# Adapter gating in a cross-attention and feed-forward kernel: once for both batches, with A through DRAM and the sums written from GpSimd's queue

## The chip, the core and the metric

The kernel runs on one core of a Trainium2 chip. The metric is the device time of one execution in microseconds (us), median of several. The engines are TensorE (PE, with its weight loads PEld), VectorE (DVE), ScalarE (ACT), GpSimd (POOL) and SyncE (SP). Each works through its own list of instructions in order, and they wait for each other by semaphores. SP, ACT and POOL can also issue DMAs; 16 DMA engines carry them all.

## What is computed

For two batches of 1024 tokens by 2048 features, all float32:

```python
x = x + fake_quant(layernorm(x)) @ fake_quant(ctx)              # ctx: 2048 x 2048 per batch
z = layernorm(x)                                                # viewed as 8 groups of 256 tokens
A_eff = einsum('bn,nri->bri', gate, lora_A)                     # gate 8 x 16, lora_A 16 x 32 x 2048
B_eff = einsum('bn,nor->bor', gate, lora_B)                     # lora_B 16 x 2048 x 32
x = x + z @ kernel + bias + (z @ A_eff.T) @ B_eff.T + (z @ A_sh.T) @ B_sh.T
```

There are eight groups of tokens (`GB` = 8), four to a batch (`GPB` = 4), and each has its own gate. So each has its own sums over the 16 adapters, `A_eff` and `B_eff` (32 x 2048). The change concerns how these sums are formed and moved.

## The kernel before

The kernel does one batch (`for b in range(B)`) after the other. A batch has two halves.

**Attention half.** The tokens of a group, two tiles of 128, are `y[g]`. `prep_x` (L277) normalises and quantises a tile and transposes it into `c1T[g]`. The context is worked in four blocks `n` of 512 columns. SP loads it in pieces of 512 KB into the small buffers `lit` (ten of 512 KB). `quantise` (L310) turns a piece into bf16 in `c2[n]`: ACT writes an int16 buffer `q2b` (three of them, L314), DVE clips it into a big buffer (L317), and the `lit` buffer goes back. `column_term` (L327) forms a correction for the block (`pcp` and `pc` on PE). `xattn_pair(b, n, g)` (L350) is a pair of tiles against a block: ACT starts the two halves of a PSUM tile `pa` with the column term (L359), PE adds 2 x 16 matmuls (L361), and DVE adds the result to `y` (L370) and takes its statistics (L372). Three such PSUM tiles go round.

**Adapters.** The adapters lie with 16 adapters x 8 ranks on 128 rows, so that `gmat`, 128 rows by (group, rank), sums over the adapters in one matmul. `gated` (L376) does this for one batch and one block of 512 columns: two loaded buffers of two pieces each, four matmuls with 32 columns of weights (4 groups x 8 ranks) into four row ranges of one PSUM tile `pg` (L383), and a copy into a `q2b` buffer by DVE (L395). Then `lora_a_step` (L398) transposes the sums on PE (`pga`, four transposes, L403), and DVE copies them into `acat` (L406), the weights of the later product `px`. `lora_b_step` (L411) writes the sums to DRAM, `bd[b]`, by eight DMAs of 32 KB on SP's queue (L416). Both are done for each batch, A for block 0 to 3 and then B for block 0 to 3. The A steps stand between the quantises of block 2 and the pairs of block 2. B step 0 stands ahead of the pairs of block 3 and the others between them. The PSUM pool `ps_m` has two buffers; `pg`, `pga`, `pcp`, `pc`, `ptz`, `pt` and `px` take turns in it.

The pieces of context and adapters come in one list, `todo`, in the order of use. Each time a buffer of `lit` is given back, `load_next` issues the next ones of the list on SP, up to nine ahead, and not those of batch 1 before batch 0's last stage.

**Feed-forward half.** When the pairs of block 3 are through, `prep_z` (L422) normalises `y` into z (DVE, L428), transposes it (PE, `ptz`, L432; ACT copies, L433) and stores it to DRAM. `lora_ax` (L442) multiplies z with `acat` (PE, `px`, L448, two tiles of 64 columns; ACT copies it to `axT`, L456). Then z times `kernel` runs as a fast matrix product: seven outer products of sums of blocks, each of seven inner ones (L611, the matmuls `fu`, `fv`, `fw`). The sums of weights are DVE's (L551, L560), those of z POOL's. Between them `Delta.step` (L466) adds the adapters' second product: ACT loads `bp` from `bd` (L473) and a row of `bias` into the one buffer `bias_b` (L476), starts a PSUM tile `pl` from it (L478), PE adds `axT` times `bp` (L483) and DVE adds that to `y` (L493).

In the last outer product of batch 0 the first stages of batch 1 are put between the inner products (`meanwhile`, L803).

A scheduler orders each engine's instructions from the dependencies and its own costs; only the DVE instructions that pass through `line` (L499) are held in the written order.

Of the kernel before, what the change touches and what calls it, by code (L numbers as in the profile page):

```python
# [10 lines left out]
F32 = mybir.dt.float32  # L11
# [55 lines left out]
def tile_quant_xattn_then_lora_ffn(  # L67
# [30 lines left out]
    H = D // 2  # L98
    KH = KT // 2
    KQ = KT // 4  # L100
    GP = GPB * RC

    const = ctx.enter_context(tc.tile_pool(name="const", bufs=1))
    small = ctx.enter_context(tc.tile_pool(name="small", bufs=4))
# [15 lines left out]
    bp = Bufs([const.tile([P, NB], F32, tag=f"bp{i}", name=f"bp{i}") for i in range(2)])  # L120
    bias_b = Bufs([const.tile([P, NB], F32, tag=f"bias{i}", name=f"bias{i}") for i in range(1)])
    axT = const.tile([P, GPB // 2, GT], F32, tag="axT", name="axT")
    gmat = const.tile([P, 2, GPB // 2, RC], F32, tag="gmat", name="gmat")
    st1 = const.tile([P, MT, NN, 6], F32, tag="st1", name="st1")
    st2 = const.tile([P, MT, NN, 6], F32, tag="st2", name="st2")
    r_s = const.tile([P, MT], F32, tag="r_s", name="r_s")
# [4 lines left out]
    ]  # L131


    bd = [dram.tile([GPB, 2, R, D], F32, tag=f"bd{b}", name=f"bd{b}") for b in range(B)]

    def bf(t, n):

# [2 lines left out]
    def flat(t):  # L140
        return t.rearrange("p k n -> p (k n)")
# [14 lines left out]
    for b in range(B):  # L156
        for n in range(2):
            todo.extend((b, raw_src(b, n, r)) for r in range(KT // 2))
        for n in range(2, 4):
            for r in range(KT // 2):  # L160
                todo.append((b, raw_src(b, n, r)))
                if r in ((3, 7) if n == 2 else (5, 7)):
                    todo.extend((b, ad_src(la, 2 * (n - 2) + r // 6 if n == 3 else r // 4, h)) for h in range(2))
        for n in range(NN):
            todo.extend((b, ad_src(lb, n, h)) for h in range(2))
    loaded = deque()
    ahead = [2]
# [14 lines left out]
    def next_loaded():  # L182
        return loaded.popleft()
# [59 lines left out]
    )  # L243
    gval = const.tile([P, GB], F32, tag="gval", name="gval")
    nc.vector.tensor_tensor(gate_b, gate_b, m_ad.unsqueeze(1).to_broadcast([P, GB, NL]), ALU.mult)
    for b in range(B):
        for i in range(2):
            nc.vector.tensor_reduce(
                gval[:, ds(b * GPB + i * 2, 2)], gate_b[:, b * GPB + i : (b + 1) * GPB : 2, :], AX.X, ALU.add
            )  # L250

    def norm_stats(stats, name):
# [68 lines left out]

    colt = {}
    pairs = []

    def column_term(b, n, c2):  # L327

# [21 lines left out]
    def xattn_pair(b, n, g, c1T, c2):  # L350

        cols = ds(n * NB, NB)
        pairs.append((b, n, g))
        pa = ps_acc.tile([P, MG, NB], F32, tag=("acc0", "acc1", "delta")[len(pairs) % 3], name=f"pa_{b}_{n}_{g}")
        for j in range(MG):

            m = g * MG + j
            with tc.high_priority():
                nc.scalar.activation(pa[:, j, :], colt[n], AF.Identity, bias=r_s[:, m : m + 1])  # L359
            for k in range(KT):  # L360
                nc.tensor.matmul(  # L361
                    pa[:, j, :],
                    c1T[g][:, k, ds(j * P, P)],
                    c2[k // 8][:, k % 8, :],
                    start=False,
                    stop=(k == KT - 1),
                    skip_group_check=True,
                )
        yp = y[g][:, :, cols]
        summed = nc.vector.scalar_tensor_tensor(yp, pa, s12, yp, ALU.mult, ALU.add)  # L370
        for j in range(MG):
            nc.vector.bn_stats(st2[:, g * MG + j, n, :], y[g][:, j, cols])  # L372
        return summed


    def gated(nm):  # L376

        ps = ps_m.tile([P, NB], F32, tag="pm", name=f"pg_{nm}")
        for h in range(2):
            buf, t = next_loaded()  # L380
            for c in range(2):
                row = (2 * h + c) * GP
                nc.tensor.matmul(  # L383
                    ps[row : row + GP, :],
                    gmat.rearrange("p i a r -> p (i a r)"),
                    t[:, c, :],
                    start=True,
                    stop=True,
                    skip_group_check=True,
                )  # L390
            lit.give(buf)
            load_next()
        st = q2b.take()
        sf = st.rearrange("p k n -> p (k n)").bitcast(F32)
        nc.vector.tensor_copy(sf, ps)  # L395
        return st, sf

    def lora_a_step(b, n):  # L398

        st, sf = gated(f"a{b}_{n}")  # L400
        pt = ps_m.tile([P, KQ, P], F32, tag="pm", name=f"pga_{b}_{n}")
        for k in range(KQ):
            nc.tensor.transpose(pt[:, k, :], sf[:, ds(k * P, P)], ident)  # L403
        q2b.give(st)
        for g in range(GPB):
            nc.vector.tensor_copy(  # L406
                acat[:, ds(n * KQ, KQ), own_col[g], :].rearrange("p k (c r) -> p k c r", c=NC),
                pt.rearrange("p k (c i a r) -> p i a k c r", c=NC, i=2, r=RC)[:, g % 2, g // 2],
            )

    def lora_b_step(b, n):  # L411

        st, sf = gated(f"b{b}_{n}")
        for c in range(NC):
            for i in range(2):
                nc.sync.dma_start(  # L416
                    out=bd[b][i::2, i, ds(c * RC, RC), ds(n * NB, NB)],
                    in_=sf[ds(c * GP + i * (GP // 2), GP // 2), :],
                )
        q2b.give(st)  # L420

    def prep_z(b, m, zq, wk):  # L422

# [34 lines left out]
    class Delta:  # L458
# [7 lines left out]
        def step(self):  # L466
            if not self.units:
                return
            pr, n, j = self.units.popleft()
            cols = ds(n * NB, NB)  # L470
            if j == 0:
                self.bp, self.bb = bp.take(), bias_b.take()
                nc.scalar.dma_start(  # L473
                    out=self.bp, in_=bd[self.b][ds(2 * pr, 2), :, :, cols].rearrange("g s r n -> (g s r) n")
                )
                nc.scalar.dma_start(out=self.bb, in_=bias[cols].partition_broadcast(P))  # L476
            pl = ps_acc.tile([P, 2, NB], F32, tag="delta", name=f"pl_{self.b}_{n}_{pr}_{j}")
            nc.scalar.copy(pl, self.bb.unsqueeze(1).to_broadcast([P, 2, NB]))  # L478

            for h in range(2):  # L480
                for i in range(2):
                    rows = slice(i * 2 * R, (i + 1) * 2 * R)
                    nc.tensor.matmul(  # L483
                        pl[:, i, ds(h * (NB // 2), NB // 2)],
                        axT[rows, pr, ds(j * P, P)],
                        self.bp[rows, ds(h * (NB // 2), NB // 2)],
                        start=False,
                        stop=True,
                        skip_group_check=True,
                    )  # L490
            for i in range(2):
                yb = y[2 * pr + i][:, j, cols]
                line(nc.vector.tensor_add(yb, pl[:, i, :], yb))  # L493
            if j == MG - 1:
                bp.give(self.bp)
                bias_b.give(self.bb)
# [194 lines left out]
            big.give(t)  # L691

    for b in range(B):
        nc.vector.tensor_tensor(
            gmat.rearrange("p i a r -> p (i a) r"),
            m_rk.unsqueeze(1).to_broadcast([P, GPB, RC]),
            gval[:, ds(b * GPB, GPB)].unsqueeze(2).to_broadcast([P, GPB, RC]),
            ALU.mult,
        )
        if b == 0:  # L700
            open_c2(0)
            prep_x(0, 0, c1T, wk)
# [21 lines left out]
        for g in range(2, GPB):  # L724
            for m in range(g * MG, (g + 1) * MG):
                with tc.issue_after(opened.ins):
                    prep_x(b, m, c1T, wk)
            for n in range(2):
                xattn_pair(b, n, g, c1T, c2[n])
                if g + 1 == GPB:  # L730
                    close_c2(n)
                    open_c2(n + 2)
                    bp.give(colt.pop(n))
                    if n == 0:
                        for r in range(NR):
                            quantise(c2[2], r)
                            if r % 4 == 3:
                                lora_a_step(b, r // 4)
                        column_term(b, 2, c2[2])
        if b == 0:  # L740
            for pr in range(GPB // 2):
                nc.sync.dma_start(out=acat[:, :, 3 * pr + 1, :], in_=a_sh)
            for bb in range(B):
                for g in range(GPB):
                    nc.sync.dma_start(out=bd[bb][g, 1 - g % 2], in_=b_sh)
        for g in range(GPB):
            xattn_pair(b, 2, g, c1T, c2[2])
            for r in {0: range(3), 1: range(3, 6), 2: range(6, 8), 3: ()}[g]:
                quantise(c2[3], r)
            if 1 <= g <= 2:  # L750
                lora_a_step(b, g + 1)
            if g == 2:
                column_term(b, 3, c2[3])
        lora_b_step(b, 0)
        close_c2(2)
        bp.give(colt.pop(2))
        first = Operands(b, 0)
# [2 lines left out]
        for g in range(GPB):  # L760
# [7 lines left out]
                first.comb("t1", "b12", "b11", ALU.subtract)  # L768
            elif g == 2:
                first.load("b22")  # L770
            if g < 3:
                lora_b_step(b, g + 1)
            if g > 0:
                zqs[g - 1] = [lit.take() for _ in range(4)]
                group_z(b, g - 1, wk, zqs[g - 1])
# [134 lines left out]
```

## Time and profile before

| | us |
|---|---|
| median of three runs (1127.28 to 1128.93) | 1128.51 |
| the profiled execution | 1128.61 |
| its span, first to last instruction | 1126.8 |
| PE busy in the span | 1072.4 |
| DVE busy | 741.5 |
| POOL busy | 266.6 |
| ACT busy | 261.1 |

The granted TensorE clock was 0.999 over the span. The profile is of one execution; a time in it is counted from the span's start. Batch 0's attention half lies at about 0 to 210 us, its adapter steps at 104 to 191; batch 1's from about 590, its adapter steps at 644 to 729. A row of the groups by line gives line, engine, operation, output<-input, size and count, then busy time and mean duration of one, then the idle time before them and what ended it. A row of a timeline begins with start and length. One float32 matmul leaves two records. The chain of waits is followed back from the last instruction to what released each step.

### The profile page before, as it was taken

The page shows a single profiled execution, that of the slowest core. Times are in us where ns is not written, and L with a number is a line of the kernel's source. Part 1 is how long each engine was busy: PE and PEld are TensorE (multiplying, and loading weights), DVE is VectorE, ACT ScalarE, POOL GpSimd, SP SyncE. Part 2 cuts the span into 40 slices and gives each one's busy share as a digit, 9 for nine tenths or more (in the row PEclk, how much of TensorE's full clock was granted, in tenths as well). Part 3 has the DMA queues.
Part 4 walks back from the last instruction along what each step waited for, and adds up shares of the span by engine and source line. Part 5 has one row for each costly group of instructions (what it writes and reads, how often), then busy time and mean ns, then how long its engine had stood idle before and what let it go on. Part 6 is the DMA issues. An engine that isn't in the chain of part 4 may idle for free.

```text
span 1126.8 us, 10619 instructions
## 1 busy us (share of the span) xinstructions
PE 1072.4 (95%) x3926; PEld 489.3 (43%) x3926; DVE 741.5 (66%) x969; ACT 261.1 (23%) x342; POOL 266.6 (24%) x106
## 2 busy tenths in 40 slices
PE   1689899999999999999999999999999999999998
PEld 0244334554444444444444433455444444444443
DVE  4685547576696768568777654766668586865861
ACT  5875513320001010001375761232000000000000
POOL 0000000234253422525000000022535343243600
PEclk9999999999999999999999999999999999999999
DMA  8991935885789757489857094588668875749611
GB/s 307 391 244 35 282 124 217 298 322 205 246 285 377 266 181 264 141 301 355 285 184 228 1 277 154 182 301 314 244 215 293 295 255 181 256 145 322 213 38 56
DMA packets 120772, 261.35 MB, mean 232 GB/s; under 512 B 11920, under 2 KB 16144, under 8 KB 119568
## 3 DMA queue, kind: packets, MB, share of 16 engines
q1 hardware_dynamic: 99264, 218.65, 56.6%
q10 hardware_dynamic: 21456, 42.02, 10.5%
q8 instruction: 31, 0.51, 0.2%
q14 instruction: 21, 0.17, 0.0%
HBM read 224.99 MB, written 37.75 MB: 233 GB/s over the span
## 4 chain that ended last, share of the span: by engine, by line
PE 80%; DMA 7%; DVE 6%; ACT 4%; issue 1%; SPq 1%; ACTq 0%; DVEq 0%
PE fu L611 33%; PE fv L611 17%; PE pa L361 13%; PE fw L611 9%; DMA lit<-in_ctx_dram 4%; PE pl L483 3%; PE ptz L432 2%; DVE big L560 1%; PE pg_a L383 1%; DVE st L283 1%; PE pg_b L383 1%; ACT big L298 1%; ACT big L295 1%; DMA bd<-q2b 1%; DMA big<-in_w_dram 1%
## 5 line engine op out<-in xcount | busy, mean ns | idle before, releaser
L611 PE MATMUL fu<-big,lit 128*128 128x512 f32 x896 | 396.3, 594 | 2.4 <-DVE y L629 2.4
L560 POOL TENSOR_TENSOR lit<-lit,lit 128x1024 f32<-128x1024 f32 x56 | 165.2, 2957 | 539.4 <-PE pa L361 209.1
L611 PEld LDWEIGHTS fu<-big,lit 128*128 128x128 f32 x896 | 167.8, 190 | 208.2 <-issue 206.7
L361 PE MATMUL pa<-big,big 128*128 128x512 bf16 x1024 | 238.0, 382 | 11.9 <-ACT pa L359 10.6
L611 PE MATMUL fv<-big,lit 128*128 128x512 f32 x448 | 198.1, 594 | 0.0
L551 POOL TENSOR_TENSOR lit<-lit,lit 128x1024 f32<-128x1024 f32 x40 | 100.9, 2524 | 283.4 <-DMA lit<-zs 255.5
L560 DVE TENSOR_TENSOR big<-big,big 128x2048 f32<-128x2048 f32 x56 | 159.4, 2850 | 5.9 <-PE ptz L432 5.3
L361 PEld LDWEIGHTS <-big 128*128 128x128 bf16 x1024 | 97.0, 98 | 146.5 <-issue 44.3
L629 DVE TENSOR_TENSOR y<-y,fu 128x1024 f32<-128x1024 f32 (+1 forms) x98 | 113.7, 1194 | 67.2 <-PE fu L611 66.8
L611 PEld LDWEIGHTS fv<-big,lit 128*128 128x128 f32 x448 | 84.3, 190 | 105.0 <-issue 105.0
L629 DVE TENSOR_TENSOR y<-y,fv 128x1024 f32<-128x1024 f32 x48 | 56.8, 1218 | 91.1 <-PE fv L611 91.1
L478 ACT COPY pl<-bias 128x1024 f32<-128x1024 f32 x32 | 32.6, 1017 | 344.9 <-DVE y L493 327.1
L314 ACT ACTIVATE q2b<-lit,sc,inv 128x1024 int16<-128x1024 f32 x64 | 76.6, 1230 | 146.4 <-DMA lit<-in_ctx_dram 124.7
L551 DVE TENSOR_TENSOR big<-big,big 128x2048 f32<-128x2048 f32 x40 | 101.7, 2544 | 13.2 <-DMA big<-in_w_dram 13.2
L611 PE MATMUL fw<-big,lit 128*128 128x512 f32 x224 | 100.6, 596 | 0.1
L370 DVE SCALAR_TENSOR_TENSOR y<-pa,k_s,y 128x1024 f32<-128x1024 f32 x32 | 41.0, 1282 | 69.7 <-PE pa L361 69.7
L359 ACT ACTIVATE pa<-bp,r_s 128x512 f32<-128x512 f32 x64 | 42.8, 684 | 105.6 <-PE pa L361 60.5
L629 DVE TENSOR_TENSOR y<-y,fw 128x1024 f32<-128x1024 f32 x24 | 28.4, 1217 | 52.5 <-PE fw L611 52.5
L611 PEld LDWEIGHTS fw<-big,lit 128*128 128x128 f32 x224 | 41.3, 190 | 48.7 <-issue 48.2
L303 PE MATMUL pt<-ident_h,big 128*128 128x128 bf16 x256 | 20.3, 231 | 29.6 <-ACT big L298 29.4
L283 DVE BATCH_NORM_STATS2 st<-y 128x6 f32<-128x512 f32 x64 | 42.1, 680 | 2.9 <-DMA y<-in_x_dram 2.9
L317 DVE TENSOR_SCALAR big<-q2b 128x1024 bf16<-128x1024 int16 x64 | 27.6, 440 | 23.7 <-ACT q2b L314 20.5
(79 smaller groups left out, 609.9 us busy)
## 6 DMA issues: line engine op xcount, KB each, us to landing
big<-in_w_dram SPq DMA_DIRECT2D x96, 1024.0 KB
lit<-zs SPq DMA_DIRECT2D x88, 512.0 KB
lit<-in_ctx_dram SPq DMA_DIRECT2D x64, 512.0 KB
out_dram<-y ACTq DMA_DIRECT2D x30, 512.0 KB
zs<-lit ACTq DMA_DIRECT2D x24, 512.0 KB
y<-in_x_dram SPq DMA_DIRECT2D x8, 1024.0 KB
lit<-in_lora_a_dram SPq DMA_DIRECT2D x32, 256.0 KB
lit<-in_lora_bt_dram SPq DMA_DIRECT2D x32, 256.0 KB
```

The source lines that it names most:

```text
L283: nc.vector.bn_stats(st1[:, m, n, :], ym[:, ds(n * NB, NB)])
L314: nc.scalar.activation(qi, t, AF.Relu, bias=z2, scale=inv2)
L317: nc.vector.tensor_scalar(c2[r // 4][:, ds(2 * (r % 4), 2), :], qi, QMAX, CENTRE, ALU.min, ALU.subtract)
L359: nc.scalar.activation(pa[:, j, :], colt[n], AF.Identity, bias=r_s[:, m : m + 1])
L361: nc.tensor.matmul(pa[:, j, :], c1T[g][:, k, ds(j * P, P)], c2[k // 8][:, k % 8, :], start=False, stop=(k == KT - 1), skip_group_check=True,)
L370: summed = nc.vector.scalar_tensor_tensor(yp, pa, s12, yp, ALU.mult, ALU.add)
L478: nc.scalar.copy(pl, self.bb.unsqueeze(1).to_broadcast([P, 2, NB]))
L483: nc.tensor.matmul(pl[:, i, ds(h * (NB // 2), NB // 2)], axT[rows, pr, ds(j * P, P)], self.bp[rows, ds(h * (NB // 2), NB // 2)], start=Fal ...
L551: line(eng.tensor_tensor(got[0], got[0], got[1], ALU.add if terms[1][2] > 0 else ALU.subtract))
L560: line(eng.tensor_tensor(out_t, at[p], at[q], op))
L611: nc.tensor.matmul(ps[:, m, :], at[:, k, ds(m * P, P)], bt[:, k, :], start=(opens and k == 0), stop=(ends and k == KQ - 1), skip_group_che ...
L629: line(nc.vector.tensor_tensor(yp, yp, chains[chain][:, js, :], ALU.add if sign > 0 else ALU.subtract))
```

## The change

- `gmat` holds the gates of all eight groups (`GP` is now 8 x 8 = 64) and is formed once, ahead of the loop over batches.
- `gated` works on half a block column, one loaded buffer: two matmuls with 64 columns of weights into the two halves of a PSUM tile (L388), one copy by DVE (L399), four DMAs of 64 KB on POOL's queue (L402).
- The copy goes no longer to a `q2b` buffer, but to one of two buffers of their own, `stage`: `bias_b`'s one buffer and `axT`, whose own work begins later.
- Both A and B are gated in batch 0 alone, for both batches. The second batch's adapter loads leave `todo`.
- The sums of A go to a DRAM tensor `ad`. In each batch, ACT's queue loads them back (`load_at`, two loads of 512 KB, L422) into a `lit` buffer, and `lora_at_step` transposes them on PE (16 transposes a batch, as before) and copies them into `acat` (L437, 8 copies a batch where there were 16 of half the size). The transposes are held behind the last matmul of the latest pair.
- `bd` is one tensor for both batches. It takes the same bytes in 32 DMAs instead of 64.

```diff
...
     KQ = KT // 4
-    GP = GPB * RC
+    GP = GB * RC
...
     axT = const.tile([P, GPB // 2, GT], F32, tag="axT", name="axT")
-    gmat = const.tile([P, 2, GPB // 2, RC], F32, tag="gmat", name="gmat")
+
+    stage = Bufs([bias_b.spare[0], axT.rearrange("p g t -> p (g t)")])
+    gmat = const.tile([P, 2, GB // 2, RC], F32, tag="gmat", name="gmat")
...
-    bd = [dram.tile([GPB, 2, R, D], F32, tag=f"bd{b}", name=f"bd{b}") for b in range(B)]
+    ad = dram.tile([2, GB // 2, R, D], F32, tag="ad", name="ad")
+    bd = dram.tile([GB, 2, R, D], F32, tag="bd", name="bd")
...
                 todo.append((b, raw_src(b, n, r)))
-                if r in ((3, 7) if n == 2 else (5, 7)):
+                if b == 0 and r in ((3, 7) if n == 2 else (5, 7)):
                     todo.extend((b, ad_src(la, 2 * (n - 2) + r // 6 if n == 3 else r // 4, h)) for h in range(2))
-        for n in range(NN):
+        for n in range(NN if b == 0 else 0):
...
     nc.vector.tensor_tensor(gate_b, gate_b, m_ad.unsqueeze(1).to_broadcast([P, GB, NL]), ALU.mult)
-    for b in range(B):
-        for i in range(2):
-            nc.vector.tensor_reduce(
-                gval[:, ds(b * GPB + i * 2, 2)], gate_b[:, b * GPB + i : (b + 1) * GPB : 2, :], AX.X, ALU.add
-            )
-
+    for i in range(2):
+        nc.vector.tensor_reduce(gval[:, ds(i * GB // 2, GB // 2)], gate_b[:, i::2, :], AX.X, ALU.add)
+    nc.vector.tensor_tensor(
+        gmat.rearrange("p i a r -> p (i a) r"),
+        m_rk.unsqueeze(1).to_broadcast([P, GB, RC]),
+        gval.unsqueeze(2).to_broadcast([P, GB, RC]),
+        ALU.mult,
+    )
...
     pairs = []
+    last_mm = []
...
             for k in range(KT):
-                nc.tensor.matmul(
+                mm = nc.tensor.matmul(
...
                 )
+        last_mm.append(mm)
...
-    def gated(nm):
+    def gated(nm, n, h, dst):
         ps = ps_m.tile([P, NB], F32, tag="pm", name=f"pg_{nm}")
-        for h in range(2):
-            buf, t = next_loaded()
-            for c in range(2):
-                row = (2 * h + c) * GP
-                nc.tensor.matmul(
-                    ps[row : row + GP, :],
-                    gmat.rearrange("p i a r -> p (i a r)"),
-                    t[:, c, :],
-                    start=True,
-                    stop=True,
-                    skip_group_check=True,
-                )
-            lit.give(buf)
-            load_next()
-        st = q2b.take()
-        sf = st.rearrange("p k n -> p (k n)").bitcast(F32)
+        buf, t = next_loaded()
+        for c in range(2):
+            nc.tensor.matmul(
+                ps[c * GP : (c + 1) * GP, :],
+                gmat.rearrange("p i a r -> p (i a r)"),
+                t[:, c, :],
+                start=True,
+                stop=True,
+                skip_group_check=True,
+            )
+        lit.give(buf)
+        load_next()
+        sf = stage.take()
         nc.vector.tensor_copy(sf, ps)
-        return st, sf
-
-    def lora_a_step(b, n):
-
-        st, sf = gated(f"a{b}_{n}")
-        pt = ps_m.tile([P, KQ, P], F32, tag="pm", name=f"pga_{b}_{n}")
-        for k in range(KQ):
-            nc.tensor.transpose(pt[:, k, :], sf[:, ds(k * P, P)], ident)
-        q2b.give(st)
-        for g in range(GPB):
-            nc.vector.tensor_copy(
-                acat[:, ds(n * KQ, KQ), own_col[g], :].rearrange("p k (c r) -> p k c r", c=NC),
-                pt.rearrange("p k (c i a r) -> p i a k c r", c=NC, i=2, r=RC)[:, g % 2, g // 2],
-            )
-
-    def lora_b_step(b, n):
-
-        st, sf = gated(f"b{b}_{n}")
-        for c in range(NC):
+        for c in range(2):
             for i in range(2):
-                nc.sync.dma_start(
-                    out=bd[b][i::2, i, ds(c * RC, RC), ds(n * NB, NB)],
+                nc.gpsimd.dma_start(
+                    out=dst[i][:, ds((2 * h + c) * RC, RC), ds(n * NB, NB)],
...
                 )
-        q2b.give(st)
+        stage.give(sf)
+
+    def lora_a_step(n):
+
+        for h in range(2):
+            gated(f"a_{n}_{h}", n, h, ad)
+
+    def lora_b_step(n):
+
+        own = [bd[i::2, i] for i in range(2)]
+        for h in range(2):
+            gated(f"b_{n}_{h}", n, h, own)
+
+    def load_at(b, n2):
+
+        buf = lit.take()
+        nc.scalar.dma_start(
+            out=flat(buf),
+            in_=ad[:, ds(b * GPB // 2, GPB // 2), :, ds(2 * n2 * NB, 2 * NB)].rearrange("i a r n -> i (a r) n"),
+        )
+        return buf
+
+    def lora_at_step(b, n2, buf, behind):
+
+        t = flat(buf)
+        for n in range(2):
+            pt = ps_m.tile([P, KQ, P], F32, tag="pm", name=f"pga_{b}_{n2}_{n}")
+            with tc.issue_after(behind):
+                for k in range(KQ):
+                    nc.tensor.transpose(pt[:, k, :], t[:, ds((n * KQ + k) * P, P)], ident)
+            for pr in range(GPB // 2):
+                nc.vector.tensor_copy(
+                    acat[:, ds((2 * n2 + n) * KQ, KQ), 3 * pr : 3 * pr + 3 : 2, :],
+                    pt.rearrange("p k (i a r) -> p a k i r", i=2, r=R)[:, pr],
+                )
+        lit.give(buf)
...
                 nc.scalar.dma_start(
-                    out=self.bp, in_=bd[self.b][ds(2 * pr, 2), :, :, cols].rearrange("g s r n -> (g s r) n")
+                    out=self.bp, in_=bd[ds(self.b * GPB + 2 * pr, 2), :, :, cols].rearrange("g s r n -> (g s r) n")
...
     for b in range(B):
-        nc.vector.tensor_tensor(
-            gmat.rearrange("p i a r -> p (i a) r"),
-            m_rk.unsqueeze(1).to_broadcast([P, GPB, RC]),
-            gval[:, ds(b * GPB, GPB)].unsqueeze(2).to_broadcast([P, GPB, RC]),
-            ALU.mult,
-        )
...
                             quantise(c2[2], r)
-                            if r % 4 == 3:
-                                lora_a_step(b, r // 4)
+                            if b == 0 and r % 4 == 3:
+                                lora_a_step(r // 4)
...
                 nc.sync.dma_start(out=acat[:, :, 3 * pr + 1, :], in_=a_sh)
-            for bb in range(B):
-                for g in range(GPB):
-                    nc.sync.dma_start(out=bd[bb][g, 1 - g % 2], in_=b_sh)
+            for g in range(GB):
+                nc.sync.dma_start(out=bd[g, 1 - g % 2], in_=b_sh)
...
                 quantise(c2[3], r)
-            if 1 <= g <= 2:
-                lora_a_step(b, g + 1)
+            if b == 0 and 1 <= g <= 2:
+                lora_a_step(g + 1)
+            if g == 2:
+                at0 = load_at(b, 0)
...
                 column_term(b, 3, c2[3])
-        lora_b_step(b, 0)
+        lora_at_step(b, 0, at0, last_mm[-1].ins)
+        if b == 0:
+            lora_b_step(0)
...
                 first.load("b22")
-            if g < 3:
-                lora_b_step(b, g + 1)
+            if g == 0:
+                at1 = load_at(b, 1)
+            if g == 1:
+                lora_at_step(b, 1, at1, last_mm[-1].ins)
+            if b == 0 and g < 3:
+                lora_b_step(g + 1)
...
```

Line numbers of the instructions that the change adds (L388, L399, L402, L422, L437) are those of the changed kernel; all others are of the kernel before.

## The prediction

> **What bounds the kernel now.** I read the page's first two parts, then TensorE's (PE's) timeline around the adapter steps, then busy time by stage, the chain of waits and SyncE's (SP's) timeline.
>
> From the page:
>
> ```profile
> PE 1072.4 (95%) x3926; PEld 489.3 (43%) x3926; DVE 741.5 (66%) x969; ACT 261.1 (23%) x342; POOL 266.6 (24%) x106
> ...
> L383 PE MATMUL pg_a<-lit,gmat 128*32 128x512 f32 x64 | 14.8, 605 | 0.0
> L383 PE MATMUL pg_b<-lit,gmat 128*32 128x512 f32 x64 | 14.8, 605 | 0.0
> ```
>
> PE is 95% busy; no other engine passes 66%. So PE time taken off comes off the end, unless the next matmul then waits. (The L383 rows are from the groups by line. They overlap, so their 14.8 us are not PE's time; starts are.)
>
> PE's timeline, batch 1's first two A steps, then B step 3:
>
> ```profile
> 644.07 1.04 PE L383 MATMUL pg_a<-lit,gmat 128*32 128x512 f32 x2
> 645.04 3.63 PE L361 MATMUL pa<-big,big 128*128 128x512 bf16 x16
> 648.60 1.06 PE L383 MATMUL pg_a<-lit,gmat 128*32 128x512 f32 x6
> 649.59 2.33 PE L361 MATMUL pa<-big,big 128*128 128x512 bf16 x10
> ...
> 652.29 1.06 PE L383 MATMUL pg_a<-lit,gmat 128*32 128x512 f32 x8
> 653.29 1.47 PE L361 MATMUL pa<-big,big 128*128 128x512 bf16 x6
> ...
> 728.31 1.07 PE L383 MATMUL pg_b<-lit,gmat 128*32 128x512 f32 x8
> ```
>
> An f32 matmul leaves two records. One alone (x2) holds PE 645.04-644.07 = 0.97 us, three (x6) 0.99, four (x8) 1.00: 32-column tiles run beside each other, so the price is per group, about **0.98 us**. Each batch has 14 groups (A 7, B 7): 13.7 us.
>
> Busy time by stage (columns: stage, length, PE, PEld, DVE, ACT, POOL busy, granted clock, DMA share, GB/s):
>
> ```profile
> 116.00:134.00 18.00, 15.84 (x84) 6.91 (x83) 9.48 (x19) 11.59 (x13) 0.00 (x0) 1.00 1.06 282
> 134.00:155.00 21.00, 21.00 (x108) 8.10 (x106) 9.71 (x19) 1.81 (x3) 0.00 (x0) 1.00 0.55 149
> 155.00:179.00 24.00, 24.00 (x107) 8.29 (x105) 13.00 (x25) 4.91 (x9) 0.00 (x0) 1.00 0.52 192
> 656.00:672.00 16.00, 15.91 (x85) 6.81 (x83) 9.63 (x19) 11.56 (x13) 0.00 (x0) 1.00 1.06 286
> 693.00:717.00 24.00, 24.00 (x107) 8.44 (x106) 13.07 (x25) 4.91 (x9) 0.00 (x0) 1.00 0.54 193
> ```
>
> From 134 us and in all of batch 1 PE is full. Only at 116-134 are the DMA engines full (1.06) and PE waits: 2.16 us at 128.83, for ACT's second start of pa, which stands behind a quantise that waits for ctx. DVE is at 46 to 54% in these stages. POOL has nothing until about 200 us.
>
> **Batch 1, removed.** Its 32 gated matmuls, 8 copies (L395, 0.68 us) and 32 bd writes go: **-13.7 us** of PE. Its 8.4 MB of adapter loads go too; they only shared full DMA engines where PE did not wait (656-672). The 16 transposes of A stay (0.53 us a group of four, before and after). What is late next, from the built order of the changed kernel:
> - pcp of block 2 now stands right behind pa of pair (0,3), cut in 10+2+2+2 between pa. Such cuts of two cost 0.33 us at 595.31 (0.98 uncut at 656.28): +0.8, and +0.3 for block 3 (10+6). The quantises of 646-653 (ACT 1.16 apiece) and the statistics between them make PE wait some 1.2 us where 0.78 are idle now: +0.4.
> - PE's 1.09 us at 750.72 waits for axT, which ACT copies only after bp's load, which waits for the bd writes. No writes, no wait: -1.1. Cutting one pl in four: +0.3.
>
> Batch 1: -13.7+0.8+0.3+0.4-1.1+0.3 = **-13.0 us** (ends -11 and -14).
>
> **Batch 0, added.** (a) Two 64-column tiles replace four 32-column ones. That they run side by side, px shows (64 columns, two at a time):
>
> ```profile
> 232.64 0.43 PE L448 MATMUL px<-lit,acat 128*64 128x256 f32 x1
> 232.65 0.43 PE L448 MATMUL px<-big,acat 128*64 128x256 f32 x1
> ```
>
> The built order gives 11 slots for A (a pair, or a lone half) and 8 for B; consecutive pairs cost 0.87 each, the others 0.98: 10.6+7.5 = 18.1 us, against 13.7: +4.4, shared out below. The number of PSUM copies does not change (16 in all, now all here): +5.4 us of DVE, in its gaps of about 4 us ahead of y at L370.
>
> (b) The sums are written from POOL: 64 DMAs of 64 KB, four behind each copy, and a buffer's next copy (DVE, in order) waits until its four have landed. Behind that copy stand y's sums, quantises and z's halves on DVE, and with them PE's PSUM buffers. No row shows a DMA issued by POOL. Nearest rows, SP's own writes of these sums and two landings in the chain of waits:
>
> ```profile
> L416 SPq DMA_DIRECT2D bd<-q2b x64: 567/567/814, 161.9 to 743.7; - x64
> ```
>
> ```profile
> 724.27 2.64 DMA zs<-lit
> 727.54 6.01 DMA bd<-q2b
> ```
>
> Issue d: ends 0.35 (ACT's bp<-bd, 346 ns) and 3.9 us (SP's two acat<-in_a_sh in 7.85); the nearest row is 0.567 for 16 rows of 2 KB, and 32 rows are written now. I take 1.0, towards its double. Landing L: 2.6 to 6.0; I take 3.5.
> - A, blocks 0 and 1 (104-134). The third copy waits for the first's four: 110.9+4x1.0+3.5 = 118.4 instead of 113; pcp waits 2 us. But ACT's second start of pa now stands behind both late ctx quantises: 129.36+1.24+0.69 = 131.3 instead of 128.83, which covers that wait and the three slots added there. So +2.5, and 0.4 for two pa less done ahead: **+2.9**. Ends 0 and +6.5: 1.05 MB of sums at 282 GB/s are 3.7 us more on full DMA engines.
> - A, blocks 2 and 3: 4.8 us of slots for 3.9: **+0.9**. The load of A on ACT's queue waits for the last A write; PE has 15.6 us of work until it needs the starts behind it: nothing, unless 8d+L passes 15.
> - B (155-194): slots **+0.6**. 32 DMAs x 1.0 = 32 us fit into 39, but steps come in pairs: the last copy needs the DMAs of the pair before, 8d+L = 11.5 us after their copy, when PE has some 10 us of work between; the bias load on ACT then waits for 4d+L. Together **+3** (ends 0 at d = 0.57 and L = 2.6, +9 at 1.13 and 6.0).
> - SP's 32 bd writes no longer stand ahead of w's loads (SP, 192.52 for 13.51 us), nor ahead of axT (PE's 1.22 us at 212.47): **-0.4**, since POOL's may be as late.
>
> Batch 0: 2.9+0.9+0.6+3-0.4 = **+7.0 us** (ends +1 and +15).
>
> **Sum.** -13.0+7.0 = -6.0. The profiled execution took 1128.61 us, 1.81 around its span of 1126.8, and is 0.1 above the median of the three (1128.51): **1122.5 us**.
>
> **A rule that speaks against it.** The quantise L317 takes 440 ns for 1024 elements, z's L428 0.72 to 0.81 us; about 0.5 us of every 4 on DVE is of this kind here. The Trainium skill, "SBUF — State Buffer", on the "DVE blocks DMA" trap, says that a DMA issued from GpSimd has its descriptors written by GpSimd's cores, which DVE locks out during its two-port modes; its example goes from about 620 to 3100 ns. By that example for every DMA, an estimate, B alone would take 32x3.1 = 99 us, and the kernel would be some 60 us slower. The page "DMA: Bandwidth & Descriptors", section "Anatomy of one DMA — SWDGE (gpsimd) path", fits 2.0 us plus bytes/436e3, so 2.15 us for 64 KB: by it as L the sum would be about 2 us lower. No row here shows either.
>
> **Rivals.**
> - *All waits hidden* (24%). DVE's gaps and POOL's idle queue speak for it, the pairs against. B's 3 us vanish and axT's 1.2 go: 2.9+0.9+0.6-1.2 = +3.2, so -9.8: **1118.8**.
> - *Given back in batch 0* (13%): L = 6.0, as the bd row has it, with full engines: A 5.5+0.9, B 7.5 with its slots, no relief: -13+13.9: **1129.5**.
> - *POOL's queue is the bound: slower* (10%). 32 DMAs must pass in B's 39 us, so it decides from d = 1.22, and eats the gain from about 1.4. At three of SP's issues, 1.7 us: 32x1.7-39 = 15.4, on top of A's 3.8 and B's slots 0.6: -13+4.4+15.4: **1135.4**. For it: software's price is unseen; against: nothing else runs on POOL, and SP's 0.567.
> - *Halves run one after the other* (3%): 32x0.87 = 27.8 instead of 18.1: -6+9.7: **1132.3**. px speaks against it. That batch 1 keeps gated matmuls is excluded: its built order has none.
>
> **Numbers.** Forecast 50%, the rivals 24, 13, 10, 3. About 0.2%, 2.3 us, is what a measurement of this kernel can tell from no change. Faster: 50+24 = 74%; same 13; slower 13. The range leaves out most of POOL's case and the tip of the hidden one: 1117 to 1131.
>
> **What shows it.** Right: no L388 matmul after 200 us; 19 slots of 0.87 to 0.98 before; batch 1 from first A step to px some 13 us shorter; the second start of pa near 131; the B stretch 2 to 5 us longer. Wrong: POOL's DMAs over 1.2 us each, DVE's L399 copies waiting many us for DMA with PE idle behind them, or new idle time of PE in batch 1 behind ACT or DVE.

## The result and the profile after

The changed kernel takes **1143.36 us** (median of 4 runs, 1142.28 to 1144.34) against 1128.72 for the kernel before in the same session: a ratio of 1.0131 (95% interval 1.0117 to 1.0144). It is slower by 14.6 us; 6 us faster was forecast. The profiled execution has a span of 1140.5 us, 13.7 more than before.

The first lines of the page of the changed kernel: the engines' busy time, the granted clock and the DMA engines' share in 40 slices of 28.5 us.

```profile
PE 1074.3 (94%) x3862; PEld 494.9 (43%) x3862; DVE 740.1 (65%) x950; ACT 261.6 (23%) x342; POOL 302.5 (27%) x170
...
PEclk9899999899999999999999999999999999999999
DMA  8981945669678965669977220687768875749511
```

PE has 64 matmuls fewer (3862 instead of 3926) and yet 1.9 us more busy time. That points to slower matmuls, and the clock row shows where one stretch of them lies: the eighth slice, 200 to 228 us, is below 9. (So is the second, where PE waits for the first loads anyway.)

PE's timeline of batch 0's adapter steps, the lines with idle time ahead of them (in brackets, and what ended it):

```profile
120.51 1.51 PE L339 MATMUL pcp<-big,ones_h 128*32 128x512 bf16 x16 [3.41 <-DVE bias L399]
169.04 1.94 PE L435 MATMUL pga<-ident,lit 128*128 128x128 f32 x8 [3.65 <-DMA lit<-ad]
189.29 5.25 PE L367 MATMUL pa<-big,big 128*128 128x512 bf16 x16 [3.80 <-ACT pa L365]
221.86 1.09 PE L453 MATMUL ptz<-ident,big 128*128 128x128 f32 x4 [4.22 <-DVE r_z L268]
```

Four waits, 15.1 us, where the kernel before had 0.78, 2.16 and 1.22. And 16 matmuls of pa take 5.25 us at 189.29, not the usual 3.6. The four microseconds behind each of the four waits (columns as in the stage table of before; the granted clock is the third from the end):

```profile
120.50:124.50 4.00, 3.99 (x22) 1.58 (x22) 2.01 (x4) 2.18 (x2) 2.41 (x5) 0.57 1.06 296
169.00:173.00 4.00, 3.96 (x16) 2.64 (x17) 2.60 (x6) 0.17 (x1) 0.00 (x0) 0.61 0.77 282
189.30:193.30 4.00, 4.00 (x12) 1.46 (x11) 2.78 (x6) 0.00 (x0) 2.46 (x5) 0.58 0.36 107
221.80:225.80 4.00, 3.94 (x15) 2.91 (x16) 2.28 (x9) 1.17 (x2) 0.00 (x0) 0.50 0.95 229
```

PE is busy in them at 0.50 to 0.61 of its clock: 4 x (0.43 + 0.39 + 0.42 + 0.50) = **7.0 us** lost on top of the waits. Before, behind the wait of 2.16 us, the clock stayed:

```profile
128.80:132.80 4.00, 3.97 (x19) 1.84 (x19) 0.74 (x2) 1.24 (x1) 0.00 (x0) 1.00 1.07 284
```

So batch 0 nearly adds up: waits 17.5 (the four, and 0.78, 0.76 and 0.84) less 4.2 before, clock 7.0, slots 4.4: 24.7 us. The second px starts at 257.50 instead of 232.64, 24.9 later. Batch 1 gives 11.1 back (24.8 us late at its pair (0,3), 13.7 at the end).

The chain of waits (start, length, what) through the second half of it:

```profile
153.39 15.51 DMA lit<-ad
169.04 1.94 PE pga L435 x8
170.98 3.02 PE pa L367 x11
176.06 1.51 POOL bd L402 x3
177.81 8.13 DMA bd<-bias
...
208.23 10.37 DMA big<-in_w_dram
218.70 2.29 DVE big L572
```

Three transfers set the pace: the load of A, the landing of B's sums, and w. The load is odd: 512 KB in 15.5 us, while a context piece of the same size lands in a median of 7.6 (8.2 between 104 and 165 us). The DMA rows from 154.5 to 163 us, while it ran (queue, kind: packets, MB, share of 16 engines):

```profile
q0 software_dynamic: 603, 0.51, 21.6%
q10 hardware_dynamic: 81, 0.33, 10.8%
```

q10 is ACT's queue: a share that stays at 10.8% of 16 engines is 1.7 engines. The engines were not full; the load did not use them. POOL's writes (issue line: min/median/max ns; then landing):

```profile
L402 POOL DMA_DIRECT2D ad<-bias x16: 588/590/727, 110.5 to 156.3; - x16
...
DMA to landing us min/median/max: 2.5/6.5/9.0
```

```profile
DMA to landing us min/median/max: 2.4/5.3/9.0
```

(The 32 writes of A's sums, then the 32 of B's.) Issue is cheap, 0.59 us; landing is long.

### The profile page after: what moved, and what is told of

It is laid out like the page before. It is cut to its first block, busy times and chain, and to the rows that moved or that the text cites. A ratio compares the mean times of both kernels' runs of the same rounds, so it can differ in the third digit from the quotient of the medians.

```text
span 1140.5 us, 10470 instructions
## 1 busy us (share of the span) xinstructions
PE 1074.3 (94%) x3862; PEld 494.9 (43%) x3862; DVE 740.1 (65%) x950; ACT 261.6 (23%) x342; POOL 302.5 (27%) x170
## 3 DMA queue, kind: packets, MB, share of 16 engines
q10 hardware_dynamic: 21976, 44.11, 11.2%
q0 software_dynamic: 5120, 4.22, 1.3%
## 4 chain that ended last, share of the span: by engine, by line
PE 81%; DVE 8%; DMA 5%; ACT 3%; issue 1%; POOL 0%; SPq 0%; DVEq 0%; ACTq 0%
PE fu L632 33%; PE fv L632 16%; PE pa L367 14%; PE fw L632 8%; PE pl L504 3%; PE ptz L453 2%; DVE st L288 2%; DMA big<-in_w_dram 1%; DMA lit<-ad 1%; PE px L469 1%; DVE big L581 1%; ACT big L300 1%; DVE y L377 1%; DMA lit<-in_ctx_dram 1%; DVE big L449 1%
## 5 line engine op out<-in xcount | busy, mean ns | idle before, releaser
L367 PE MATMUL pa<-big,big 128*128 128x512 bf16 x1024 | 242.9, 389 | 13.3 <-ACT pa L365 12.0
L367 PEld LDWEIGHTS <-big 128*128 128x128 bf16 x1024 | 99.7, 100 | 146.7 <-issue 45.6
L572 DVE TENSOR_TENSOR big<-big,big 128x2048 f32<-128x2048 f32 x40 | 99.0, 2476 | 13.1 <-DMA big<-in_w_dram 13.1
L402 POOL DMA_DIRECT2D ad<-bias x16 | 9.6, 606 | 134.5 <-DVE bias L399 134.5
## 6 DMA issues: line engine op xcount, KB each, us to landing
y<-in_x_dram SPq DMA_DIRECT2D x8, 1024.0 KB, 13.1
```

The source lines that it names most:

```text
L367: mm = nc.tensor.matmul(pa[:, j, :], c1T[g][:, k, ds(j * P, P)], c2[k // 8][:, k % 8, :], start=False, stop=(k == KT - 1), skip_group_chec ...
L572: line(eng.tensor_tensor(got[0], got[0], got[1], ALU.add if terms[1][2] > 0 else ALU.subtract))
```

## The experiments

Each was measured beside the kernel before, whose median was 1127.99 to 1129.27 us by group. Ratios are to that, with 95% intervals. Single runs of one kernel lie 2 to 12 us apart, so a difference of some 1 us between two rows shows nothing. Four edits recur; as short diffs on the changed kernel:

```diff
# load: A's sums in DRAM by (group, rank), one run of 128 equal steps for a batch
-ad = dram.tile([2, GB // 2, R, D], ...)
+ad = dram.tile([GB, R, D], ...)
-gated(..., ad)
+gated(..., [ad[i::2] for i in range(2)])
-in_=ad[:, ds(b * GPB // 2, GPB // 2), :, cols].rearrange("i a r n -> i (a r) n")
+in_=ad[ds(b * GPB, GPB), :, cols].rearrange("g r n -> (g r) n")
# split: gmat's columns by (i, rank, pair), so a write's outer step is 8 ranks, not 4 groups
-gmat = const.tile([P, 2, GB // 2, RC], ...)
+gmat = const.tile([P, 2, RC, GB // 2], ...)
-out=dst[i][:, ranks, cols]
+out=dst[i][:, ranks, cols].rearrange("a r n -> r a n")
# late A: its loads behind ctx of block 3 (r = 2, 5, 7), its steps behind pairs (2,0), (2,1), (2,2)
-if b == 0 and r % 4 == 3:
-    lora_a_step(r // 4)
+for na in {0: (0,), 1: (1,), 2: (2, 3), 3: ()}[g]:
+    lora_a_step(na)
# order: w's sum for b22 behind the normalise of z's second group, batch 0 only
-first.block("b22")
+with tc.issue_after(last_z[0]):
+    first.block("b22")
```

| run | edits | us | ratio |
|---|---|---|---|
| e1_load16 | load | 1135.22 (1129.6 to 1141.7) | 1.0063 (1.0045 to 1.0081) |
| e2_stage6 | buffers | 1143.03 | 1.0131 (1.0114 to 1.0148) |
| e3_both | load, buffers | 1134.34 | 1.0066 (1.0043 to 1.0089) |
| e4_sp | SP's queue | 1155.86 | 1.0249 (1.0234 to 1.0264) |
| e5_b_early | e3, B early | 1131.29 | 1.0026 (1.0007 to 1.0044) |
| e6_a_late | e3, late A | 1129.62 | 1.0021 (1.0002 to 1.0040) |
| e7_k8 | e3, split | 1127.01 | 0.9986 (0.9972 to 1.0000) |
| e8_a_late_b1 | e6, B one place early | 1136.60 | 1.0081 (1.0054 to 1.0108) |
| e9_k8_only | split | 1137.95 | 1.0083 (1.0062 to 1.0104) |
| e10_a_late_k8 | e6, split | 1129.21 | 1.0014 (0.9994 to 1.0034) |
| e11_a_late_k8_z_first | e10, order past group 3 | 1140.67 | 1.0112 (1.0090 to 1.0134) |
| e12_k8_z_first | e7, order past group 3 | 1142.64 | 1.0130 (1.0114 to 1.0145) |
| e13_k8_z1 | e7, order | 1124.72 | 0.9965 (0.9950 to 0.9980) |
| e14_a_late_k8_z1 | e10, order | 1122.67 | 0.9952 (0.9936 to 0.9968) |
| e15_z1_only | order | 1140.47 | 1.0108 (1.0082 to 1.0134) |
| **e16_a_late_k8_2buf_z1** | load, split, late A, order | **1121.72** | 0.9942 (0.9924 to 0.9959) |
| e17_without_split | e16 less split | 1126.56 | 0.9977 (0.9966 to 0.9989) |
| e18_without_load16 | e16 less load | 1137.23 | 1.0068 (1.0046 to 1.0091) |

**Load, buffers, queue.** The edit for the buffers gives the copies the quarters of the working buffer `wk` in A and three `q2b` in B:

```diff
+for u in range(4):
+    stage.give(flat(wk)[:, ds(u * NB, NB)])
```

> Only the order of the rows of A's sums in DRAM changes (group, rank instead of half, pair, rank), so that the load back is one run of 128 equal steps instead of 2 x 64. Theory one (the load lit<-ad runs on about 2 of the 16 DMA engines: its packets took 10 to 11% of the engines' time from 154 to 167 us, 130 packets, landing after 15.5 us): landing falls to 3 to 6 us, PE's idle of 3.65 us at 169 and the 3.4 us at half clock behind it go, about -5.5 us: 1136 to 1139. Rival (the load is late because it waits for the sums' writes, or for its first bytes to be readable): landing stays above 12 us, 1142 to 1145.

> The writes stay on GpSimd's queue; the copies get six buffers for A (four quarters of the working buffer that prep_x has left) and five for B (three of q2b), instead of two. Theory one (batch 0's loss is DVE's copy standing behind the landing of a buffer's last four writes): PE's idles of 3.41 us at 120.5 and 3.80 us at 189.3 go, with about 1.8 us of half clock behind each: -8 to -11 us, 1132 to 1136. Rival (the writes themselves are too slow for the stretch, whatever the buffers): the waits move to the load of A and to bp, less than 3 us gained, 1140 or more.

> e1 and e2 together. Theory one: both terms add, -14 to -17 us: 1126 to 1130, with only DVE's wait for w (4.2 us at 221.9) and the 4.4 us of added slots left of batch 0's loss. Rival: no more than the better of the two alone.

e1 shows the first theory right. Landing falls from 15.51 to 3.9 us; the DMA rows of e1 from 156 to 160 us:

```profile
q10 hardware_dynamic: 144, 0.52, 40.9%
...
lit<-ad ACTq DMA_DIRECT2D x1, 512.0 KB, 3.9
```

The same bytes take 41% of the engines' time in 4 us instead of 11% in 15. Nothing but the order of rows has changed, so waiting for the writes was not the cause. PE's wait of 3.65 us for the load is gone. The time falls by 8.1 us, more than the 5.5 foretold. (The profiled execution was the slowest of the ten, 1141.65 us; it serves here for the load alone.)

A rule for this stands in the Trainium skill, "DMA: Bandwidth & Descriptors", section "Why a DMA increments its semaphore by 16 and not by 1": a DMA is split over the largest number of engines, up to 16, that divides the slowest dimension of both its sides. By it 2 x 64 rows go over 2 engines and 128 over 16. The rows agree (1.7 engines; then a landing a quarter as long). So do the packets on ACT's queue: the load as changed has 130 (153.4 to 168.9 us), in e1 144, which is 2 and 16 beyond its 128 rows. Which engines they were, no run here shows.

e2 refutes the theory on the buffers, and with it what I had read off the idle lines. DVE's wait ahead of pcp goes, and PE waits as long a little later, by e2's timeline:

```profile
129.39 7.67 PE L368 MATMUL pa<-big,big 128*128 128x512 bf16 x27 [3.92 <-ACT pa L366]
```

```profile
115.13 12.31 DMA lit<-in_ctx_dram
127.53 1.24 ACT q2b L320
129.39 7.67 PE pa L368 x27
```

(The second fence is its chain of waits.) At 116 to 130 us the DMA engines are full (1.07 in the changed kernel); the sums compete with the context there, and with more buffers a context transfer of 12.31 us is what PE waits for.

e3 gains 0.9 us on e1 (1134.34 against 1135.22), so its rival is right: the two terms do not add.

> The changed kernel, with the sums' writes issued by SP instead of GpSimd; the same two buffers. Theory one (landing is slow because of few DMA engines and busy queues, not because software writes the descriptors): landing stays at 4 to 7 us, the same idles of PE remain and w's loads stand behind the writes in addition: 1142 to 1150. Rival (GpSimd's queue is what is slow): landing falls to 2.5 to 3.5 us and most of batch 0's loss goes: 1125 to 1134.

Neither: 12.5 us slower than the changed kernel. Where the chain has a landing of SP's writes it is 4.63 to 6.16 us, as theory one has it. But w's loads now wait in SP's order behind the writes, which costs more than it says (18.45 and 14.09 us in the chain for two of them). Yet at pair (2,3) e4 is 3.2 us *ahead* of the kernel before. SP, in order, issues the adapters' loads behind the copies that its writes wait for, and the DMA engines' share at 116 to 130 us is 0.89 (1.07 in the changed kernel). That pointed at A's place. It does not clear GpSimd's queue in this stage: the same edit takes packets away (80 for each write from GpSimd, 36 from SP, by the queues' counts). But e16, below, beats both kernels with GpSimd's queue, so the loss did not need another.

```diff
-nc.gpsimd.dma_start(out=dst[i]...
+nc.sync.dma_start(out=dst[i]...
```

**Place and split.** How late y's pairs are against the kernel before (start of DVE's sum of the pair in the profiled executions, us):

| pair | changed | e3 | e7 | e13 | e16 | e18 |
|---|---|---|---|---|---|---|
| (0,3) | -0.7 | -1.0 | -1.7 | -1.7 | -3.0 | -2.8 |
| (2,0) | +3.8 | +3.5 | +1.1 | +1.2 | -7.7 | -7.0 |
| (2,3) | +5.5 | +6.0 | +3.6 | +3.7 | -1.9 | -1.3 |
| (3,0) | +10.4 | +7.1 | +3.9 | +3.4 | -0.1 | +13.1 |
| (3,2) | +17.9 | +10.0 | +7.1 | +7.0 | +2.1 | +15.7 |
| (3,3) | +25.4 | +17.7 | +10.2 | +7.6 | +3.0 | +16.8 |
| batch 1, (0,0) | +24.9 | +17.2 | +8.7 | +7.2 | +4.0 | +17.0 |

The columns differ already at (0,3), ahead of the first adapter step, by up to 2.3 us; why is not known. So what a stage costs is the difference of two rows: from (0,3) to batch 1 the changed kernel loses 25.5 us, e16 7.0.

> e3_both (1134.3), with B's four steps two places earlier: behind pairs (2,2) and (2,3) and ahead of and behind pair (3,0), so that they stand ahead of z's halves and w's sums on DVE instead of between them. Theory (what is left of the loss behind 165 us, 1.93 us idle at 192.6, 4.12 at 213.9 and the half clock behind it, comes from B's copies and z's sharing DVE's order with the sums that wait for w): most of these 8 us go, 1126 to 1130. Rival (DVE waits for w because w's load can only be issued when pair (3,2) is done): the wait of some 5 us at L573 stays, 1133 to 1136.

> e3_both (1134.3), with A's first two steps and their loads moved from the ctx quantises of block 2's input (104 to 130 us, DMA engines full) to behind pairs (2,0) and (2,1), the others behind (2,2). Theory (the first stage's loss is DMA bandwidth: 2 MB of A's loads and 0.5 MB of sums ahead of ctx): the idle of 4.97 us at 130.7 goes, the first pair of block 2 ends no later than before's 132.5, -5 to -8 us: 1126 to 1130. Rival (the loss is only put off: the load of A and B's steps become late instead): pair (3,0) ends as in e3 (176.1), 1133 or more.

In e3 ACT waits for a context piece in the first stage, and PE for ACT:

```profile
128.82 1.24 ACT L320 ACTIVATE q2b<-lit,sc,inv 128x1024 int16<-128x1024 f32 x1 [4.61 <-DMA lit<-in_ctx_dram]
130.69 7.67 PE L368 MATMUL pa<-big,big 128*128 128x512 bf16 x27 [4.97 <-ACT pa L366]
```

e6 shows that the first stage is bound by the DMA engines: with A out of it both waits are gone, and the sum of pair (2,0) starts 5.5 us before the kernel before's, 9 us sooner than in e3. From 116 to 130 us the engines are as full as in e3 (1.06 and 1.07), but GpSimd's writes take 5.3% of them, not 23.3. Of this lead of 9 us 4.7 us remain at the end; this wait takes the rest:

```profile
209.33 1.09 PE L455 MATMUL ptz<-ident,big 128*128 128x128 f32 x4 [6.04 <-DVE r_z L270]
```

e5 gains 3.0, between the two theories: DVE's wait of 5.3 us for w stays, B's copies only move.

```diff
# e5: B's steps two places earlier (e8, on e6: one place)
+if b == 0 and g >= 2:
+    lora_b_step(g - 2)
```

> e6 with B's steps one place earlier as well (behind (2,3), ahead of block 3, behind (3,0) and (3,1)). Theory: both terms add: 1119 to 1125, faster than the kernel before. Rival (the stage from 165 us is bound by w's loads whatever stands on DVE): as e6, 1127 to 1131.

e8 refutes that the two add up: 7 us slower than e6, with two waits of 5 us (212.3 and 233.2) behind sums that wait for w. Why B's steps one place earlier cost that much was not followed up.

> e3_both (1134.3), with the rows of the sums in rank-major order, so that each write's outer step in DRAM is 8 ranks instead of 4 groups; sizes and number of writes stay. If a 64 KB write's landing (medians 4.1 and 4.8 us in e3) is set by the number of DMA engines that it is split over, it falls to 3 to 3.5 us and the time by 1 to 2 us: 1132 to 1133.5. Rival (it is set by what else is queued on the engines): landing 4 to 5 us as now, 1133.5 to 1135.5.

> The changed kernel (1143.4) with e7's rank-major rows alone: writes split 8 ways instead of 4, still two buffers and the load of A still on about 2 engines. Theory (the writes lie on few of the 16 engines and so hold up the ctx and w loads, whose every share must land): part of e7's 7 us comes here too, 1136 to 1140. Rival (the split helps only once buffers and load are mended): 1142 to 1144.

The split gives 7.3 us on e3, more than either side foretold, 5.4 alone, as its theory had it, and 4.8 in e16 (e17 below; 4.0 by the ratios), but nothing on e6 (e10 below). On e3 it is not by way of the landing: that goes from medians of 5.4 and 3.9 us (A's writes, B's) to 5.8 and 4.3. What gets shorter are the longest waits for other transfers: ACT's for the context 4.6 to 2.9 us, DVE's for w 5.3 to 3.4. That fits writes that lie on few engines and hold up the one share of a big transfer that must still land. No view here shows single engines, so this cause is argued, not shown. By the page's rule the writes go from 4 engines to 8; no run here shows that number. And the split changes something else too: GpSimd's 64 writes have 3072 packets instead of 5120, the issue of one takes 0.54 us instead of 0.59, and A's sums (2.1 MB) take 9.8% of the engines' time from 104 to 165 us, not 11.9 as in e3. No run separates fewer packets from more engines.

**The order of w's sum.** What is left in e7 and e10 is a wait on DVE's order. In the changed kernel:

```profile
208.24 1.28 DVE L377 SCALAR_TENSOR_TENSOR y<-pa,k_s,y 128x1024 f32<-128x1024 f32 x1 [0.75 <-PE pa L367]
209.44 0.80 DVE L449 TENSOR_SCALAR big<-y,mv_z,rstd_z 128x1024 f32<-128x1024 f32 x1
...
218.70 2.29 DVE L572 TENSOR_TENSOR big<-big,big 128x2048 f32<-128x2048 f32 x1 [5.38 <-DMA big<-in_w_dram]
220.91 0.81 DVE L449 TENSOR_SCALAR big<-y,mv_z,rstd_z 128x1024 f32<-128x1024 f32 x1
```

The half at 220.91 is the last of z's second group. px (7 us of PE) needs it, and it stands behind a sum that waits for w. The kernel before waits for w too, but there the second group's last half stands ahead of the sum, and px runs meanwhile, from 202.29:

```profile
199.56 0.81 DVE L428 TENSOR_SCALAR big<-y,mv_z,rstd_z 128x1024 f32<-128x1024 f32 x1 [0.52 <-PE ptz L432]
202.81 2.29 DVE L551 TENSOR_TENSOR big<-big,big 128x2048 f32<-128x2048 f32 x1 [2.44 <-DMA big<-in_w_dram]
```

In the changed order, with the added copies in it, the sum has slipped ahead of that half.

> e6 (A's steps late, 1129.6) with e7's 8-way writes. If the two mend different things (e6 the ctx loads at 104 to 130 us, e7 the loads behind it too), 1122 to 1126. If both mend only the first stage, 1127 to 1130.

> e10 with the sum of w's blocks for b22 (the third L572) held on DVE behind the normalise of z's third group, in whose order it stood ahead and waited for w. Theory (what is left in batch 0 is DVE's order around w's late load: 6.04 us idle at 209.3 in e6 and the half clock behind it): 4 to 8 us under e10, 1116 to 1121. Rival (w is then missed by the products at the start of the feed-forward part): within 2 us of e10.

> e7 (1127.0) with the same order on DVE, A's steps where the change put them. Theory: its idle of 2.26 us at 209 goes, 1124 to 1126. Rival: as in e11, 1126 to 1128.

e10 adds nothing to e6 (1129.2 against 1129.6), its second case: its wait at 207.6 is 6.71 us. e11 and e12 held the sum back past the *third* group, in both batches, and the rival was right and too mild: fw waits for w's sum in its turn, in e12

```profile
236.95 3.78 PE L637 MATMUL fw<-big,lit 128*128 128x512 f32 x4 [8.46 <-DVE big L577]
```

> e7 (1127.0) with the sum of w's blocks for b22 (the third L572) put on DVE behind the normalise of z's second group only, as the kernel before has it, and in batch 0 only; e12 had put it behind the third group. Theory (the change's added DVE work let that sum slip ahead of the second group's last halves, so that px, 7 us of PE, can no longer fill the wait for w): the idle of 2.26 us at 209 and what stands behind it go, 1122 to 1125. Rival (w's load is the bound, the order only says where PE waits): 1126 to 1128.

> e10 (A's steps late, 8-way writes, 1129.2) with the same order. Theory: its idle of 6.71 us at 207.6 and the half clock behind it (1.7) go, 1120 to 1123. Rival: 1127 to 1129.

> The changed kernel (1143.4) with that order alone. Theory: its idle of 4.22 us at 221.9 and the half clock behind it go, 1136 to 1139. Rival: 1142 to 1144.

> e14 with the change's own two buffers instead of six and five. If DVE's wait for the landing behind two buffers is worth little once the writes are no longer in the full stage: within 1.5 us of e14. If it decides: 3 us or more slower.

Past the second group only, as before the change, it gains 2.3 us on e7 (the intervals still touch) and 6.5 on e10, as the theories had it. Alone (e15) it is 2.9, between theory and rival, and four runs from 1138.4 to 1145.0 do not set that clear of noise. In e13 px fills the time, with no idle ahead of it:

```profile
209.16 1.67 PE L369 MATMUL pa<-big,big 128*128 128x512 bf16 x7
210.76 7.13 PE L475 MATMUL px<-lit,acat 128*64 128x256 f32 x64
```

e16 has the change's own two buffers and is no slower than e14 (1121.72 against 1122.67). It beats both kernels: 0.58% under the kernel before, 21.6 us under the changed one. (Of the 7.6 us between its profiled execution and that of before, 3.0 lie ahead of the first adapter step.) Its page:

```profile
PE 1066.3 (95%) x3862; PEld 491.0 (44%) x3862; DVE 743.8 (66%) x951; ACT 261.6 (23%) x342; POOL 299.4 (27%) x170
...
PEclk9999999999999999999999999999999999999999
```

With the same 3862 matmuls PE is busy 8.0 us less than in the changed kernel: the clock is whole.

> e16 (1121.7) with the writes 4 ways again, as the change has them; load in 128 equal steps, A late and w's sum put back stay. Theory (the split mattered in e7 because the writes met full DMA engines; A's place takes most of them out of there): 1122 to 1124. Rival (the split acts on its own): 1126 or more.

> e16 (1121.7) with the load of A on 2 x 64 steps again; split, A's place and w's sum stay. Theory (two engines take 15 us for the load wherever it stands, and PE's transposes stand in order behind it): 4 to 8 us slower than e16, 1126 to 1130. Rival (the load hides in its new place): 1121 to 1123.

Both edits count. Without the split 4.8 us come back, as the rival had it. Without the load's row order 15.5 do (14.2 by the ratios), twice what its theory had: the load takes 20.44 us there, and PE stands ahead of the transposes of A:

```profile
169.44 1.94 PE L437 MATMUL pga<-ident,lit 128*128 128x128 f32 x8 [10.83 <-DMA lit<-ad]
```

## Why the prediction was wrong

The sign was wrong, through batch 0.

- **Batch 1: right in kind, 1.9 short.** Forecast -13.0, measured -11.1. The gated matmuls, their copies and the wait for axT (1.09) went, pcp's cuts cost 0.8 as said. Two terms were too small: pl cut in four costs 4 x 0.63 - 1.07 = 1.4 (0.3 taken), and PE waits 0.51 and 1.07 for z's halves on DVE (0.33 before).
- **Slots: right.** Two 64-column tiles run side by side: a pair (four records) takes 1.08 us, two pairs on end 1.94. There are 19 slots, 18.4 us by their starts (18.1 forecast).
- **POOL's issue: too dear.** 0.59 us (1.0 taken), so that rival falls. Nor did DVE slow it: the longest issue is 0.77, where the example of the Trainium skill, "SBUF — State Buffer", that I had weighed has 3.1.
- **Landing: too short.** Medians of 6.5 and 5.3 us, up to 9.0 (3.5 taken, ends 2.6 to 6.0). The range of the row was given; I took the lower half. But e2 shows that the waits which I priced from it (pcp, the B copies) were not the price: mended, they move on.
- **A, blocks 0 to 3: 2.3 us short.** Forecast +3.8; from pair (0,3) to (2,3) 6.1 are lost. The 3.41 us ahead of pcp was to be covered by ACT's second start, but that was done at 132.48 (forecast 131.3), and PE, late and at half clock, had work until then: the wait was covered by nothing. I had named full DMA engines as the upper end; e6 shows A's place among them to be the cause.
- **"The load of A on ACT's queue waits for the last A write; PE has 15.6 us of work until it needs the starts behind it: nothing, unless 8d+L passes 15": this step failed worst.** 8d+L came to 8 x 0.59 + 6.5 = 11.2, so by its own condition it should have held. I priced when the load may start, and not how long it takes: 15.5 us, at the share of two engines. And PE's transposes, held behind the last pair of block 2, stand in its order ahead of half of pair (3,0). e1 has its price at 8.1 us, e18 at 15.5.
- **B: +3 forecast, with slots and relief +3.2; 14.4 measured** between pair (3,0) and the second px. The pairs of steps and their landings were the smaller part. Two of the four waits lie here, with 3.7 us of clock; the order of w's sum (2.3 to 6.5 us) had no term at all. I had costed DVE's added 5.4 us as lying in its gaps, and not asked what it would push past.
- **No term for the clock.** Every wait was priced at its length; four of them cost 1.6 to 2.0 us more.

The rival nearest to it, "given back in batch 0", had its place right (+13.9) and 11 us too little. The 13% for a slower kernel stood on POOL's queue as the bound, which is not how it came. The forecast, 1122.5, is about what e16 reaches (1121.7), and e16's 7.0 us in batch 0 are the forecast's, but that is luck: e16 has A in another place, the load, the split and w's sum mended. With A where the change put it, e13 comes to 1124.7, with more buffers. So batch 1's gain was real, and batch 0's price is mostly that of four stalls, not of the work moved there.

## What to carry to other kernels

Before a round trip through DRAM is costed, look at the outermost dimension of both sides of each DMA: here 2 against 128 steps made the same 512 KB take 15.5 us or 3.9, though the engines were not full. Where a moved step adds work to an engine in order, list what that engine does next, transfer by transfer: a small operation ahead of one that waits can uncover a wait that a long product used to fill. When a wait goes and the time stays, ask which resource is full there: more buffers gained 0.3 us (e2) in a stage whose DMA engines were.

## What the runs showed of the hardware

- PE's granted clock fell to about half for some 3.5 us behind waits of 2.62 us (e4, at 191.4: 0.64 over the next 4 us), 2.71 (e9, at 199.8: 0.65), 2.96 (e9, at 119.9: 0.61 from 121 to 125), 3.22 (e7, at 128.2: 0.65) and the four above, not behind 2.16 (before), 2.26 (e7), 2.52 and 2.87 (e9, at 187.5 and 221.1) and 2.94 (e5, at 128.5). The Trainium skill, "TensorE: Matmul & The Clock Gate", part 1, has an idle window of about 3.4 us for it; here it begins below 3, and from 2.6 to 2.95 waits went either way.
- A write of 64 KB issued from GpSimd costs its queue 0.59 us (0.54 with the split), as from SP (medians 0.58 to 0.61 in e4), and lands after 1.8 us (e7) to 10.5 (e2).
- Runs of one kernel with such waits can spread widely: e1 12 us over ten runs, against 3.3 over six in e16, which has none of them. That the clock is the reason is not shown.
